# A slot's products ahead of the scores and its other stages behind them, and half-size products summed whole, in a fused encoder-decoder transformer layer

## The chip, the cores and the metric

The kernel runs on one core of one Trainium2 chip. The metric is the device time of one execution in microseconds (us); before the change it is 2730.48 us, the median of three runs (2728.22 to 2731.12).

The engines named below are PE (TensorE, matmuls and transposes through an identity), PEld (its weight loads, which overlap the matmuls), DVE (VectorE), ACT (ScalarE), POOL (GpSimd) and SP (the engine that issues all DMAs). Each works through its own instructions in the order in which the program gives them.

## The reference

One pre-norm transformer layer pair in float32. The encoder works on a short context (2 batches of 77 rows, 512 wide), the decoder on 2 batches of 2048 rows. Cut to what matters:

```python
memory = encoder(ctx)                      # 77 rows a batch
yn = ln(y, n1)
y = y + mha(yn, yn, sa_in, sa_out, causal bias)      # 16 heads of 32, 2048 x 2048 scores
y = y + mha(ln(y, n2), memory, ca_in, ca_out, bias)  # 2048 x 77 scores
y = y + relu(ln(y, n3) @ ff1.T + b1) @ ff2.T + b2    # 512 -> 2048 -> 512
def mha(xq, xkv, ...):
    scores = einsum("bhqd,bhkd->bhqk", q, k) / sqrt(32) + bias
    out = softmax(scores) @ v
    return out @ w_out.T + b_out
```

## The kernel before, in words

**Two stages.** The first stage, about the first 1640 us, is the decoder's causal self-attention; the encoder and the cross-attention of the first block of rows are spread out inside it. The second stage does cross-attention and the feed-forward part. The change touches the first stage alone.

**Blocks, units, pieces.** A block is a batch b and 512 of its rows, m = 0 to 3; the eight blocks are numbered x = 4b + m. A block has 16 units: four groups g of four heads times four tiles t of 128 query rows. A unit of m sees 4m + t + 1 key tiles of 128, which are cut into pieces of at most four tiles. So a unit of m = 1 has two pieces, and one of m = 2 or 3 three or four.

**One turn of the main loop** handles up to two pieces of one unit. On PE it is: `turn` transposes the unit's probabilities (L427, one PSUM bank for each key tile, copied out by ACT at L434 or by DVE at L432); if these pieces end unit n, `slot(n + 1)` does side work; one or two pieces of the scores of a later unit (`scores`, L375: four heads, a bank each; DVE empties each bank while it takes the row maximum, at L384 and L391, and L401 joins the maxima); and `values` (L456) multiplies the turned probabilities with v. The exponentials (L406) run on ACT.

**A slot's side work.** Three tables are filled ahead of the loop. `jobs` holds the products that make q, k, v of the next block and the output projection of the last one. In blocks with m > 0 these are Strassen-Winograd products of half size, numbered 1 to 7: `pair_job` for q (a and b are the two halves of the heads, so a25 is products 2 and 5) and `part_job` for k, v and o. `light` holds stages that ran ahead of the jobs: layer-norm statistics (L282 to L286) and centring, `norm_turn` (four transposes at L305 into one bank, emptied by four ACT instructions at L310), reciprocals of the softmax sums (L482, L484), loads, and for slots 65 to 98 the stages of the first block's cross-attention (L811, L836, L866, L874, L883 on PE; L845, L846 and L884 on DVE). `late` holds stages that ran behind the jobs: encoder stages, sums on POOL (L962), stores. Slots are counted here within a block, 0 to 15; slot s of block x is `slot(16x + s)`. Norms of the next block stand in slots 5 to 10, the output projection in slots 6 to 9, the next block's q and k products in slots 11 to 15.

**Eight banks.** PSUM has eight banks of 512 columns, handed out in a ring (`bank`): every product, each transposed key tile, each head of a score piece and each norm turn takes the next one. A matmul into a bank waits until the bank's last user has been read out. What PE may start therefore hangs on what stood eight banks before it in the program's order.

**What sets the order.** The scheduling is by hand: the order of the Python calls is the order on each engine.

**Sums of products.** Each half-size product leaves 128x512 in a bank, which is added onto one or two quarters of its result (DVE, or ACT for product 1). `last[0]` is true for the last job of a slot; its sums are made in two halves of 256 columns (L1150), those of the others whole (L1159, L1161, L1164).

Of the kernel before, what the change touches and what calls it, by code (L numbers as in the profile page):

```python
# [17 lines left out]
P = 128  # L18
# [36 lines left out]
def tile_encoder_decoder(ctx: ExitStack, tc: tile.TileContext, ins, out):  # L55
# [103 lines left out]
    with (  # L159
# [252 lines left out]
        def turn(pieces):  # L412
# [10 lines left out]
            for o, load in enumerate(loads):  # L423
# [608 lines left out]
        def pair_job(b, m, h, parts):  # L1032
# [8 lines left out]
            def run(w):  # L1041
# [3 lines left out]
                mm = bank()  # L1045
                for j, i in enumerate(parts):
                    n = of_nT(b, m, PARTS[i][1])
                    for c in range(2):
                        nc.tensor.matmul(mm[:, ts(j, TOK)], w[:, 2 * j + c, :], n[:, c, :], start=c == 0, stop=c == 1)  # L1049
# [3 lines left out]
                got = [mm[:, ts(j, TOK)] for j in range(len(parts))]  # L1053
                if parts == (1, 6):
                    ve.tensor_scalar(d["11"], got[0], qbias[:, 2 * h : 2 * h + 1], None, ALU.add)
                    ve.tensor_tensor(d["12"], got[1], d["11"], ALU.add)
                elif parts == (7, 4):
                    ve.scalar_tensor_tensor(d["22"], got[0], qstep[:, h : h + 1], d["12"], ALU.add, ALU.add)
                    ve.tensor_tensor(d["21"], got[1], d["22"], ALU.add)
                elif parts == (2, 5):  # L1060
                    for to, j in (("11", 0), ("12", 1), ("22", 1)):
                        ve.tensor_tensor(d[to], got[j], d[to], ALU.add)
                else:
                    assert parts == (3,)
                    ve.tensor_tensor(d["12"], got[0], d["12"], ALU.add)

            return load, run, True
        n_tiles, last = {}, [False]
# [4 lines left out]
        ADDS = {2: ("11",), 3: ("12",), 5: ("22", "12")}  # L1073
# [34 lines left out]
        def part_job(kind, b, m, i):  # L1108
# [20 lines left out]
            def run(w):  # L1129
                n, mm = of_o(b, m, by) if kind == "o" else of_nT(b, m, by), bank()  # L1130
                left, right = (w, n) if kind == "k" else (n, w)
                for f in range(2):
                    for c in range(2):
                        nc.tensor.matmul(  # L1134
                            mm[:, ts(f, TOK)], left[:, c, ts(f, P)], right[:, c, :], start=c == 0, stop=c == 1,
                        )
                got = mm.rearrange("p (f n) -> p f n", f=2)
                d = {to: place(to) for to in ("11", "12", "21", "22")}
                if i == 1 and kind == "k":
                    for f in range(2):  # L1140
                        nc.scalar.activation(
                            d["11"][:, f, :], got[:, f, :], AF.Identity, bias=vec("dec_sa_in_b", NC + f)
                        )
                elif i == 1:
                    nc.scalar.copy(d["11"], got)
                elif last[0] and not (i == 7 and kind == "k"):
                    for f in range(2):
                        for to in {6: ("12",), 7: ("22",), 4: ("21",)}.get(i) or ADDS[i]:
                            onto = {6: "11", 7: "12", 4: "22"}.get(i, to)
                            ve.tensor_tensor(d[to][:, f, :], got[:, f, :], d[onto][:, f, :], ALU.add)  # L1150
                elif i == 6:
                    ve.tensor_tensor(d["12"], got, d["11"], ALU.add)
                elif i == 7 and kind == "k":
                    for f in range(2):
                        ve.scalar_tensor_tensor(
                            d["22"][:, f, :], got[:, f, :], kstep[:, f : f + 1], d["12"][:, f, :], ALU.add, ALU.add
                        )
                elif i == 7:
                    ve.tensor_tensor(d["22"], got, d["12"], ALU.add)  # L1159
                elif i == 4:  # L1160
                    ve.tensor_tensor(d["21"], got, d["22"], ALU.add)  # L1161
                else:
                    for to in ADDS[i]:
                        ve.tensor_tensor(d[to], got, d[to], ALU.add)  # L1164
# [20 lines left out]
        late = {n: [] for n in light}  # L1185

        for x, (b, m) in enumerate(blocks):
# [13 lines left out]
            else:  # L1201
                todo = {
                    -5: "a16 a74", -4: "k1 k6", -3: "k7 k4", -2: "k2 a25", -1: "k5 k3 a3", 0: "v1 v6", 1: "v7 v4 v2",
                    2: "v5 v3", 3: "b16", 4: "b74 b25", 5: "b3",
# [789 lines left out]
```

## Time and profile before

| what | value |
|---|---|
| median of three runs | 2730.48 us |
| the profiled execution, its own time | 2728.59 us |
| its span, first to last instruction | 2726.8 us |
| self-attention stage | 0 to about 1640 us |
| block 1 (batch 0, m = 1) | 161 to 368 us |
| block 2 (m = 2) | 368 to 597 us |
| block 3 (m = 3) | 597 to 853 us |
| block 5 (batch 1, m = 1) | 989 to 1183 us |
| block 6 (m = 2) | 1183 to 1412 us |
| block 7 (m = 3) | 1412 to 1640 us |

In the timeline view a row has the start in us, the duration in us, the engine, the line and operation, what is written and read, the shapes and a count of merged instructions; in brackets stands idle time of the engine just before, and what ended it. A float32 matmul at L375, L456 or L1134 is two instructions in the trace, a transpose at L427 is one, so a score piece is eight rows of L375. In the view by windows each row is a stretch, its length, and then each engine's busy time and instructions.

### The profile page before, as it was taken

Reading aid. Unit: us, or ns where it says so; the run is one execution under the profiler, and the core shown is the slowest. Engines: PE = TensorE matmul, PEld = TensorE weight load, DVE = VectorE, ACT = ScalarE, POOL = GpSimd, SP = SyncE. Lnnn points to the kernel's source line nnn. Section 1 sums busy time; section 2 is a strip of 40 time slices with the busy share of each in tenths; the row PEclk is TensorE's granted clock in tenths of the full one; section 3 lists DMA queues with packets and bytes.
Section 4 is the critical chain, followed back from the end, with each engine's and each line's share of the span. In section 5 each row is a group of like instructions: output and inputs, shape, how many; then the busy total and the mean of one; then the engine's idle time right before and its main releaser. Section 6 shows DMA issues by size and latency. Waiting matters only on the chain.

```text
span 2726.8 us, 68267 instructions
## 1 busy us (share of the span) xinstructions
PE 2708.1 (99%) x26606; PEld 2217.9 (81%) x26606; DVE 1839.9 (67%) x5445; ACT 1537.0 (56%) x2978; POOL 1002.4 (37%) x844
## 2 busy tenths in 40 slices
PE   9999999999999999999999999999999999999998
PEld 6678877777876677777777777898989898989898
DVE  4776688888885677788888783646464746464645
ACT  3554567777786547667777784444444444444431
POOL 2612235500300513322300203455556565656456
PEclk9999999999999999999999999999999999999999
DMA  8724355511213522343311206565657565656465
GB/s 242 213 92 135 126 155 164 168 50 43 67 45 89 143 76 72 111 133 98 126 50 35 79 19 220 171 214 173 213 171 239 168 216 170 218 166 219 151 224 185
DMA packets 296277, 385.10 MB, mean 141 GB/s; under 512 B 41184, under 2 KB 165648, under 8 KB 295826
## 3 DMA queue, kind: packets, MB, share of 16 engines
q1 hardware_dynamic: 295954, 380.73, 44.1%
q8 instruction: 211, 3.46, 0.5%
q14 instruction: 112, 0.92, 0.1%
HBM read 334.15 MB, written 46.47 MB: 140 GB/s over the span
## 4 chain that ended last, share of the span: by engine, by line
PE 95%; DVE 1%; ACT 1%; DMA 1%; POOL 1%; issue 1%; SPq 0%; DVEq 0%; POOLq 0%; ACTq 0%
PE psum L427 18%; PE psum L1638 14%; PE psum L1667 13%; PE psum L375 11%; PE psum L456 9%; PE psum L1134 8%; PE psum L1801 3%; PE psum L1758 3%; PE psum L1049 3%; PE psum L866 2%; PE psum L836 1%; PE psum L874 1%; PE psum L590 1%; PE psum L811 1%; PE psum L239 1%; PE psum L215 1%
## 5 line engine op out<-in xcount | busy, mean ns | idle before, releaser
L406 ACT ACTIVATE pp<-pp,nm 128x128 f32<-128x128 f32 (+15 forms) x512 | 611.8, 1200 | 28.6 <-DVE nm L401 27.8
L384 DVE TENSOR_SCALAR_CACHE_REDUCE pp<-psum 128x512 f32<-128x512 f32 (+3 forms) x1024 | 556.2, 591 | 51.3 <-PE psum L375 49.7
L434 ACT COPY pts<-psum 128x512 f32<-128x512 f32 x714 | 384.1, 594 | 312.6 <-PE psum L427 265.6
L427 PE MATMUL psum<-ident,pp 128*128 128x128 f32 x4352 | 530.4, 277 | 4.7 <-ACT nT L310 4.0
L427 PEld LDWEIGHTS psum<-ident,pp 128*128 128x128 f32 x4352 | 474.0, 141 | 55.7 <-DVE pp L384 21.4
L375 PE MATMUL psum<-kT,q 32*128 32x512 f32 (+3 forms) x2560 | 336.5, 559 | 2.5 <-DVE q L217 1.0
L456 PEld LDWEIGHTS psum<-pts,vv 128*32 128x32 f32 x8704 | 226.4, 110 | 127.4 <-DVE pp L384 55.4
L1667 PE MATMUL psum<-pp 128*128 128x128 f32 x2560 | 304.5, 276 | 1.9 <-POOL pp L962 1.6
L1667 PEld LDWEIGHTS psum<-pp 128*128 128x128 f32 x2560 | 296.3, 192 | 8.6 <-issue 2.8
L432 DVE COPY pts<-psum 128x512 f32<-128x512 f32 x374 | 245.2, 685 | 82.6 <-PE psum L427 80.3
L456 PE MATMUL psum<-pts,vv 128*32 128x128 f32 x8704 | 279.6, 276 | 0.8 <-DVE mx L391 0.3
L962 POOL TENSOR_TENSOR pp<-pp 128x512 f32<-128x512 f32 x159 | 212.8, 1356 | 111.0 <-DMA pp<-in_dec_ff_wT_dram 50.6
L1638 PE MATMUL psum<-vv,pp 128*128 128x256 f32 x1024 | 236.2, 381 | 0.0
L375 PEld LDWEIGHTS psum<-kT,q 32*128 32x128 f32 x2560 | 146.3, 183 | 107.1 <-issue 41.3
L1638 PEld LDWEIGHTS psum<-vv,pp 128*128 128x128 f32 x1024 | 190.3, 190 | 25.8 <-issue 0.5
L391 DVE CUSTOM_DVE_ANT_0 pp<-psum,bias 128x256 f32<-128x256 f32 (+1 forms) x512 | 196.0, 411 | 19.7 <-PE psum L375 19.7
L1651 DVE TENSOR_TENSOR kT<-kT,psum 128x512 f32<-128x512 f32 x96 | 65.8, 686 | 191.6 <-PE psum L1638 191.4
L1654 ACT ACTIVATE kT<-kT,vecs 128x256 f32<-128x256 f32 x192 | 86.9, 501 | 156.6 <-DVE kT L1651 155.9
L1638 PE MATMUL psum<-nT,pp 128*128 128x256 f32 x768 | 174.1, 380 | 0.5 <-DVE oT L471 0.5
L1638 PEld LDWEIGHTS psum<-nT,pp 128*128 128x128 f32 x768 | 144.2, 190 | 20.8 <-issue 1.4
L1675 ACT COPY oT<-psum 128x128 f32<-128x128 f32 x56 | 15.0, 268 | 238.9 <-PE psum L1667 238.9
L494 POOL TENSOR_TENSOR oT<-rirows,oT 128x512 f32<-128x512 f32 x30 | 38.4, 1280 | 293.6 <-DMA rirows<-rec 181.7
(272 smaller groups left out, 4110.6 us busy)
## 6 DMA issues: line engine op xcount, KB each, us to landing
pp<-w_d SPq DMA_DIRECT2D x520, 256.0 KB
pp<-in_dec_ff_wT_dram SPq DMA_DIRECT2D x112, 256.0 KB
bias<-tzg SPq DMA_DIRECT2D x128, 128.0 KB
pp<-wo_d SPq DMA_DIRECT2D x56, 256.0 KB
wqk<-in_dec_sa_in_wT_dram SPq DMA_DIRECT2D x52, 256.0 KB
wqk<-sa_q SPq DMA_DIRECT2D x84, 128.0 KB
vv<-in_enc_ff_wT_dram SPq DMA_DIRECT2D x8, 1024.0 KB
xr<-in_x_dram SPq DMA_DIRECT2D x32, 256.0 KB
```

The source lines that it names most:

```text
L375: nc.tensor.matmul(banks[r][:, : kn * P], q[rows4(r), ts(t, P)], kT[rows4(r), g, k0 * P : (k0 + kn) * P], start=True, stop=True,)
L384: nc.vector.tensor_scalar(p[:, k0 : k0 + far], s[:, :far], 1.0, None, ALU.mult, ALU.max, accum_out=st["mx"][:, r, c : c + 1],)
L391: nc.vector.tensor_tensor_reduce(p[:, k0 + far : i + 1], s[:, far:kn], near[:, 2 - (kn - far) :], 1.0, LOWEST, ALU.add, ALU.max, accum_out ...
L406: nc.scalar.activation(p, p, AF.Exp, bias=nm, accum_out=to)
L427: nc.tensor.transpose(pt[:, ts(x, P)], state[n]["p"][r][:, k], ident)
L432: nc.vector.tensor_copy(pts[:, : len(load), :], pt[:, :w])
L434: nc.scalar.copy(pts[:, : len(load), :], pt[:, :w])
L456: nc.tensor.matmul(ot[rows4(r)], vv[:, k, ts(g * HC + r, HD)], got.pop((n, k, r)), start=k == k0 and (whole or not begun), stop=k == k1 - ...
L962: engine.tensor_tensor(out, a, b, ALU.subtract)
L1134: nc.tensor.matmul(mm[:, ts(f, TOK)], left[:, c, ts(f, P)], right[:, c, :], start=c == 0, stop=c == 1,)
L1638: nc.tensor.matmul(mm[:, ts(f, TOK)], a[:, c, ts(f, P)], b[:, c, :], start=fresh and f == 0 and c == 0, stop=c == 1, skip_group_check=True,)
L1667: nc.tensor.matmul(psum[:, bank_i, ts(col, P)], lhs[:, c, :], w[:, c, :], start=fresh and k in (0, 3) and c == 0, stop=c == 3, skip_group_ ...
```

## The change

Three things are done at once.

1. For units of blocks with m > 0, and for the slots 10 and 11 of the very first block (`parted`), the slot is taken apart. Its jobs (`products`) stay where they were, between `turn` and the scores; its `light` and `late` stages now follow the scores and stand ahead of `values`. One stage, the second part of a weight store (`w2_store(c, 1)`), goes with the products (`ahead`).
2. Every half-size product is summed whole, behind its four matmuls, also the last one of a slot. Both the q products and the others now take their sums from one table (`SUMS`); products 2 and 5 change places (a52 for a25, b52 for b25, output 5 ahead of 2), and k's product 2 goes behind the pair a52.
3. In a `turn` whose slot has no jobs (`direct`), DVE copies every other bank of the second half, where it copied all of the second half (or banks 4 and 6 of eight), and one group of exponentials stands ahead of another copy.

The core of the diff:

```diff
-                w = len(load) * P
+                w, half = len(load) * P, len(loads) // 2
-                if free or (o % 2 if first else o in (4, 6) if len(loads) == 8 else o >= (len(loads) + 1) // 2):
+                if free or (o % 2 if first else o >= half and (len(loads) - o) % 2 if direct else o in (4, 6) if len(loads) == 8 else o >= (len(loads) + 1) // 2):
...
-                if not first and o == (7 if len(loads) == 8 else min(3, len(loads) - 1)):
+                if not first and o == (max(0, len(loads) - 2) if direct else 7 if len(loads) == 8 else min(3, len(loads) - 1)):
...
+                mm = [bank()] * 2
...
-                elif last[0] and not (i == 7 and kind == "k"):
-                    for f in range(2):
-                        for to in {6: ("12",), 7: ("22",), 4: ("21",)}.get(i) or ADDS[i]:
-                            onto = {6: "11", 7: "12", 4: "22"}.get(i, to)
-                            ve.tensor_tensor(d[to][:, f, :], got[:, f, :], d[onto][:, f, :], ALU.add)
...
+                    else:
+                        for to, onto in SUMS[i]:
+                            ve.tensor_tensor(d[to][:, f], got[:, f], d[onto][:, f], ALU.add)
...
+                sums(slice(0, 2))
...
-                    -5: "a16 a74", -4: "k1 k6", -3: "k7 k4", -2: "k2 a25", -1: "k5 k3 a3", 0: "v1 v6", 1: "v7 v4 v2",
+                    -5: "a16 a74", -4: "k1 k6", -3: "k7 k4", -2: "a52 k2", -1: "k5 k3 a3", 0: "v1 v6", 1: "v7 v4 v2",
...
-                    for k, part in ((0, 1), (0, 6), (1, 7), (1, 4), (2, 2), (2, 5), (3, 3)):
+                    for k, part in ((0, 1), (0, 6), (1, 7), (1, 4), (2, 5), (2, 2), (3, 3)):
...
+        def products(n):
+            for f in ahead[n]:
+                f()
+            for _, run, _ in jobs[n]:
+                load_next()
+                run(loaded[ran[0]])
+                ran[0] += 1
+
         def slot(n):
             for f in light[n]:
                 f()
-            for k, (_, run, _) in enumerate(jobs[n]):
-                load_next()
-                last[0] = k == len(jobs[n]) - 1
-                run(loaded[ran[0]])
-                ran[0] += 1
+            products(n)
             for f in late[n]:
                 f()
...
-            light[u + k + 2].append(lambda c=c: w2_store(c, 1))
+            ahead[u + k + 2].append(lambda c=c: w2_store(c, 1))
...
-            turn(pair)
+            parted = ends and n + 1 < end and (units[n][1] > 0 or n in (9, 10))
+            turn(pair, parted and not jobs[n + 1])
...
-            if ends and n + 1 < end:
+            if parted:
+                products(n + 1)
+            elif ends and n + 1 < end:
                 slot(n + 1)
             if not third:
                 exps((0, 2, 1, 1)[units[n][1]])
...
+            if parted:
+                for f in light[n + 1] + late[n + 1]:
+                    f()
             if third and not ends:
                 exps(1)
             values(pair)
```

Over the program DVE gets 63 additions fewer, and seven copies out of PSUM go from DVE to ACT; PE, POOL and SP have the same instructions as before. New lines: the half-size products are L1053 for q (L1049 before) and L1161 for k, v and o (L1134 before), their sums L1157.

**PE in slot 5 of block 5**, from the turn to the values; L811 is a norm's turn, L883 the output projection and L836 the scores of the first block's cross-attention, L1049 the q product 3. Before:

```order
L427 MATMUL psum<-ident,pp 128x128 x20
L811 MATMUL psum<-ident,kT 128x128 x4
L883 MATMUL psum<-vv,kT 128x512 x4
L836 MATMUL psum<-pp 128x77 x16
L1049 MATMUL psum<-nT,wqk 128x256 x2
L375 MATMUL psum<-kT,q 128x384 x4
L375 MATMUL psum<-kT,q 128x512 x4
L456 MATMUL psum<-pts,vv 32x128 x20
```

Now:

```order
L427 MATMUL psum<-ident,pp 128x128 x20
L1053 MATMUL psum<-nT,wqk 128x256 x2
L375 MATMUL psum<-kT,q 128x384 x4
L375 MATMUL psum<-kT,q 128x512 x4
L811 MATMUL psum<-ident,kT 128x128 x4
L883 MATMUL psum<-vv,kT 128x512 x4
L836 MATMUL psum<-pp 128x77 x16
L456 MATMUL psum<-pts,vv 32x128 x20
```

The three cross-attention stages went from ahead of the product to behind both score pieces. On DVE the readings of their banks (L884, L845, L846) moved with them, from ahead of the sum of the q product to behind the last reading of the score banks.

**PE in slot 9 of block 2**, output product 3 and one norm turn. Before:

```order
L427 MATMUL psum<-ident,pp 128x128 x8
L305 MATMUL psum<-ident,xt 128x128 x4
L1134 MATMUL psum<-wqk,oT 128x256 x4
L375 MATMUL psum<-kT,q 128x384 x4
L375 MATMUL psum<-kT,q 128x512 x4
L456 MATMUL psum<-pts,vv 32x128 x8
```

Now:

```order
L427 MATMUL psum<-ident,pp 128x128 x8
L1161 MATMUL psum<-wqk,oT 128x256 x4
L375 MATMUL psum<-kT,q 128x384 x4
L375 MATMUL psum<-kT,q 128x512 x4
L305 MATMUL psum<-ident,xt 128x128 x4
L456 MATMUL psum<-pts,vv 32x128 x8
```

The norm turn, and with it a bank of the ring, went from ahead of the product to between the scores and the values.

**DVE in slot 8 of block 7**: the last copies of the turn, a group's reciprocals, the sums of output products 2 and 5, and the first reading of the scores. Before:

```order
L432 COPY pts<-psum 128x512 x2
L482 RECIPROCAL ri_110<-sums 128x16
L484 STREAM_TRANSPOSE rt<-ri_110 128x32
L1164 TENSOR_TENSOR wbig<-psum,wbig 128x2x256
L1150 TENSOR_TENSOR wbig<-psum,wbig 128x256 x4
L391 ISA pp,mx<-psum,bias 128x2x128
L391 ISA mx 128x1
```

Now:

```order
L432 COPY pts<-psum 128x512 x2
L1157 TENSOR_TENSOR wbig<-psum,wbig 128x2x256 x3
L391 ISA pp,mx<-psum,bias 128x2x128
L391 ISA mx 128x1
```

The sum of the last product was four additions of 256 columns (product 5, onto two quarters) and is one of 512 (product 2); the reciprocals moved to behind the readings of both score pieces.

More of the change, by code (lines that the diff above doesn't have):

```diff
@@ L410, in tile_encoder_decoder, with turn @@
         got = {}
-        def turn(pieces):
+        def turn(pieces, direct):
             first = units[pieces[0][0]][1] == 0
@@ L1072, in tile_encoder_decoder @@
         }
-        ADDS = {2: ("11",), 3: ("12",), 5: ("22", "12")}
         def of_nT(b, m, name):
@@ L1134, in run @@
                         nc.tensor.matmul(
-                            mm[:, ts(f, TOK)], left[:, c, ts(f, P)], right[:, c, :], start=c == 0, stop=c == 1,
+                            mm[f][:, ts(f, TOK)], left[:, c, ts(f, P)], right[:, c, :], start=c == 0, stop=c == 1,
                         )
-                got = mm.rearrange("p (f n) -> p f n", f=2)
-                d = {to: place(to) for to in ("11", "12", "21", "22")}
-                if i == 1 and kind == "k":
-                    for f in range(2):
[L1141 to L1145, printed above, removed]
-                elif last[0] and not (i == 7 and kind == "k"):
-                    for f in range(2):
-                        for to in {6: ("12",), 7: ("22",), 4: ("21",)}.get(i) or ADDS[i]:
-                            onto = {6: "11", 7: "12", 4: "22"}.get(i, to)
[L1150 to L1164, printed above, removed]
+                sums(slice(0, 2))
             return load, run, True
@@ L1184, in tile_encoder_decoder @@
         light = {n: [] for n in range(-1, len(units) + NU)}
-        late = {n: [] for n in light}
+        late, ahead = {n: [] for n in light}, {n: [] for n in light}
         for x, (b, m) in enumerate(blocks):
```

65 lines of the change are left out of this document (42 added, 23 removed).

## The prediction

> **What bounds the kernel now.** I read the page's busy times first, then the windows by block, then the score matmuls alone in the same windows, then the timeline at the places where these run long.
>
> ```profile
> PE 2708.1 (99%) x26606; PEld 2217.9 (81%) x26606; DVE 1839.9 (67%) x5445; ACT 1537.0 (56%) x2978; POOL 1002.4 (37%) x844
> 368.00:597.00 229.00, 228.90 (x2800) 178.42 (x2792) 190.05 (x649) 166.76 (x286) 86.42 (x72) 1.00 0.47 143
> 989.00:1183.00 194.00, 193.93 (x2056) 146.91 (x2048) 145.28 (x497) 128.84 (x266) 55.62 (x47) 0.99 0.29 90
> 1412.00:1640.00 228.00, 227.81 (x3036) 181.94 (x3038) 191.86 (x637) 180.81 (x269) 19.02 (x15) 1.00 0.16 51
> 1900.00:2000.00 100.00, 100.00 (x732) 91.16 (x731) 48.99 (x98) 43.09 (x94) 56.34 (x52) 1.00 0.59 194
> ```
>
> The last four rows are blocks 2, 5 and 7 and a piece of the feed-forward stage; their columns are PE, PEld, DVE, ACT, POOL, granted clock, DMA share, GB/s. PE shows no idle time anywhere, and all idle time of the run would be 2726.8 − 2708.1 = 18.7 us. But a matmul's recorded time covers its wait inside the pipeline: weight loads fill 91% of the feed-forward window and 76 to 80% of the blocks. So the blocks may hold waits that the busy time hides, while DVE is at 75 to 84%.
>
> The Trainium skill says the same of such traces ("Perfetto Trace Analysis", section "Identifying the Most-Contended Engine"): matmul busy time is a bad measure because matmuls are pipelined, the share of the weight loads a good one. By busy time alone at most 18.7 us could be won; by the page more, and the next rows agree with the page.
>
> ```profile
> 161.00:368.00 207.00, 33.74 (x272) 15.21 (x272) 1.00 0.39 123
> 368.00:597.00 229.00, 53.52 (x424) 23.03 (x424) 1.00 0.47 143
> 597.00:853.00 256.00, 59.51 (x448) 26.62 (x448) 1.00 0.15 47
> 989.00:1183.00 194.00, 42.05 (x272) 17.87 (x272) 0.99 0.29 90
> 1183.00:1412.00 229.00, 53.61 (x424) 23.03 (x424) 1.00 0.33 105
> 1412.00:1640.00 228.00, 57.55 (x432) 25.95 (x432) 1.00 0.16 51
> 495.16 2.00 PE L375 MATMUL psum<-kT,q 32*128 32x512 f32 x16
> 497.09 1.96 PE L456 MATMUL psum<-pts,vv 128*32 128x128 f32 x64
> 276.29 1.78 PE L375 MATMUL psum<-kT,q 32*128 32x384 f32 x16
> 278.01 1.30 PE L456 MATMUL psum<-pts,vv 128*32 128x128 f32 x40
> ```
>
> The first six rows are the score matmuls (L375) alone by block: PE, PEld. Blocks 1 and 5 run the same 272, and block 5 takes 8.3 us more. The last rows give the price without a wait, from a pair of pieces to the values behind it: 1.93 us for two full ones, 1.72 us for one of three tiles and one of four, so 0.108 to 0.121 us a row. By these the waits are 1 to 4 us in block 1, 9 to 13 in block 5, 2 to 8 in blocks 2 and 6 each, 6 to 11 in block 3 and 5 to 11 in block 7: 25 to 55 us in all. That is the pool from which this change can draw.
>
> **Part by part. The cross-attention stages of block 5.** Slot 5 before:
>
> ```profile
> 1043.34 3.60 PE L883 MATMUL psum<-vv,kT 128*128 128x512 f32 x8
> 1046.87 1.13 PE L836 MATMUL psum<-pp 32*128 32x77 f32 x32
> 1048.10 0.48 DVE L845 TENSOR_REDUCE cmx<-psum 128x4 f32<-128x308 f32 x1 [0.42 <-PE psum L836]
> 1048.99 4.37 PE L375 MATMUL psum<-kT,q 32*128 32x384 f32 x16
> 1052.11 0.28 DVE L384 TENSOR_SCALAR_CACHE_REDUCE pp<-psum 128x128 f32<-128x128 f32 x1
> 1053.30 1.30 PE L456 MATMUL psum<-pts,vv 128*32 128x128 f32 x40
> ```
>
> The scores run from 1048.99 to 1053.30, 4.31 us where 1.72 are needed: the last heads want the four banks of L836, which DVE empties from 1048.10 on, and DVE reads no score before 1052.11. Moved behind, the product and both pieces follow the turn at once, and DVE reads scores while PE does L883 (3.60 us) and L836 (1.13 us). These and the values (1.30) give DVE 6 us for the eight heads, so neither engine waits. Gain here 2.6 us. Slots 2 and 10 have the same shape. Of the 9 to 13 us in this block I take **9**.
>
> **Norm turns in front of the scores** stand in slots 7 to 10 of blocks 1, 2, 3 and 5. Slot 9 of block 2:
>
> ```profile
> 485.99 0.60 PE L305 MATMUL psum<-ident,xt 128*128 128x128 f32 x4
> 486.87 0.68 DVE L282 BATCH_NORM_STATS2 bnst<-xt 128x6 f32<-128x512 f32 x1
> 487.59 1.53 ACT L310 ACTIVATE nT<-psum,vecs 128x128 f32<-128x128 f32 x4
> 487.87 0.15 DVE L285 TENSOR_SCALAR rstd<-bnmv 128x1 f32<-128x1 f32 x1
> 488.25 2.77 PE L375 MATMUL psum<-kT,q 32*128 32x384 f32 x16
> 488.35 0.76 DVE L1150 TENSOR_TENSOR wbig<-psum,wbig 128x256 f32<-128x256 f32 x2 [0.33 <-PE psum L1134]
> 490.94 0.64 PE L456 MATMUL psum<-pts,vv 128*32 128x128 f32 x16
> ```
>
> The scores take 490.94 − 488.25 = 2.69 us, 0.97 over the 1.72 of such a pair: a head wants the norm turn's bank, which ACT frees at 489.12. Behind the scores it hinders none, so 0.97 is the upper end. The lower is what DVE gains, since the next turn's eight banks wait for its readings: it starts about 0.43 us earlier, PE's share of the norm turn (485.99 to the product at 486.42). Of twelve such slots in blocks 1 to 3 (block 5 is counted above), near the lower end because DVE is at 83% there: 12 × 0.43 = **5**.
>
> **The very first block, slots 10 and 11.** Here the turn itself waits for the norm's bank:
>
> ```profile
> 105.60 1.48 ACT L310 ACTIVATE nT<-psum,vecs 128x128 f32<-128x128 f32 x4
> 107.14 0.86 PEld L427 LDWEIGHTS psum<-ident,pp 128*128 128x128 f32 x8 [2.07 <-ACT nT L310]
> 113.11 1.29 PEld L427 LDWEIGHTS psum<-ident,pp 128*128 128x128 f32 x12 [2.44 <-ACT nT L310]
> ```
>
> L310 stands behind four exponentials on ACT, so transposes idle 2.07 and 2.44 us. With the norm turns behind the scores, four score banks come between, and the transposes pass; the copies on ACT are as late as before and give some of it back. Of 4.5 us I take **3** (bounds 0 and 4.5). Block 1's encoder stages leave 1 to 4 us of waits; I take **1.5**.
>
> **Sums whole.** Slot 8 of block 3:
>
> ```profile
> 723.09 0.69 DVE L1164 TENSOR_TENSOR wbig<-psum,wbig 128x512 f32<-128x512 f32 x1 [0.60 <-PE psum L1134]
> 724.64 0.74 PEld L375 LDWEIGHTS psum<-kT,q 32*128 32x128 f32 x14 [0.33 <-ACT nT L310]
> 724.82 1.42 DVE L1150 TENSOR_TENSOR wbig<-psum,wbig 128x256 f32<-128x256 f32 x4 [1.03 <-PE psum L1134]
> ```
>
> The halves were meant to start before the product ends, and do not: the first starts at 724.82, behind all its matmuls, after DVE idled 1.03 us. So one whole sum loses nothing and takes 0.69 us for 0.76 (63 × 0.07 = 4.4 us of DVE, hidden; counted at 0). The new order counts for more: behind the last product stands product 2's 0.69 us in place of product 5's 1.42, so DVE reaches the scores 0.73 us earlier. That shows where the scores wait for it: two such slots of m = 3, and partly the slots 14 (k2 behind a52). I take **2.5** (bounds 0 and 5).
>
> The page "PSUM — Partial Sum Buffer" of the Trainium skill (section "PSUM bank collisions raise a hardware error") says to guard PSUM by bank, not by address; by this rule no half can be read while PE fills the other, and the 1.03 us agree. If halves could start early, the change would cost up to 0.38 us at each such sum.
>
> **What it costs.** Before, DVE did the statistics in front of the sums, in time in which it waited for products. Now they follow eight score readings and stand ahead of the next turn's copies.
>
> ```profile
> L282 DVE BATCH_NORM_STATS2 bnst<-xt 128x6 f32<-128x512 f32 x24 | 16.2, 675 | 0.0
> L482 DVE RECIPROCAL ri<-sums 128x16 f32<-128x16 f32 x28 | 6.8, 242 | 0.0
> 1122.20 1.03 PE L1049 MATMUL psum<-nT,wqk 128*128 128x256 f32 x4
> 1117.39 1.28 POOL L962 TENSOR_TENSOR xr<-nT,xt 128x512 f32<-128x512 f32 x1
> ```
>
> One set is 1.15 us (486.87 to 488.02), 24 sets 28 us. They are hidden while DVE has slack before the next scores; at 83% of a turn of about 14 us it has 2.4. Bounds 0 and 28; I charge a fifth, **5**, because DVE's idle time is spread. POOL's token sums for slot 11 start later too: the last of them ended at 1118.67, 3.5 us before the first q product at 1122.20, and out of the moved scores come 2 to 4 us; I charge **1**. SP's loads for the products now stand ahead of the slot's other DMAs, which can only help them; nothing is counted. The seven copies that go to ACT cost it 0.59 instead of 0.69 on DVE, nothing on the path.
>
> **Sum:** 9 + 5 + 3 + 1.5 + 2.5 − 5 − 1 = 15 us gained. The profiled execution (2728.59 us; its span is 1.8 less) would come to 2713.6; the median of the runs stands 1.9 above it, so I forecast 2730.5 − 15 = **2715 us**, with a range of its own of 2706 to 2722.
>
> **Rivals.** (a) *DVE sets the pace.* Where PE saves a wait, the ring makes it wait again for DVE in the next turn. For it: DVE at 83 to 84% in blocks 2, 3, 6 and 7, and the 0.43 against 0.97 above. Against it: block 5 has DVE at 75% and the largest waits. If only half of block 5's 9 and 3 of the rest stay, less 2.5 of the costs, it is 5 us: 2725.
>
> (b) *The moved statistics are exposed: slower.* One mechanism, on DVE between the last score reading and the first copy of the next turn. It decides from the point where the readings still queued when the values start, plus 1.15, outlast the values and the first four transposed tiles (1.96 + 1.8 us). Exposed in blocks 2, 3 and 6 are 12 sets of 1.15 and some 18 reciprocals with their transposes of 0.45, 22 us; the 5 and 2.5 are not gained, and of the other 13.5 all stay: 22 − 13.5 + 1 = +9.5, 2740 us. For it: eight readings of 0.61 are 4.9 us. Against it: half of them are done when the values start.
>
> (c) *More is freed.* If the pool of 25 to 55 us goes by half or more, 30 us: 2700. For it: every wait that the timeline shows has a moved stage or a sum in front. Against it: DVE's share.
>
> (d) *It does nothing to the time*, the waits only changing their place: it lies at the upper end of (a).
>
> **How the numbers follow.** Forecast 0.52, (a) and (d) 0.22, (b) 0.18, (c) 0.08. A measurement of this kernel can tell about 0.2%, 5.5 us. Faster by more: 0.52 + 0.08 and half of (a), 0.70; within: the rest of (a) and a little of (b), 0.14; slower 0.16. The range of 2702 to 2733 leaves out the far ends of (b) and (c), about 0.2.
>
> **What would show it.** In the changed trace the score matmuls of block 5 take about 33 us where they took 42.05, those of blocks 2 and 6 some 51; slot 5 of block 5 has 1.7 us from scores to L811; no transposes wait 2 us at 105 to 113 us; DVE starts one sum of 512 about 0.2 us behind each product. I am wrong if transposes of the turn (L427) or the values (L456) take up what the scores give back, as (a) and (b) say, or if slot 11 of block 5 waits for POOL's sums.

## The result and the profile after

| | median, us | lowest to highest | runs |
|---|---|---|---|
| before | 2729.44 | 2724.54 to 2731.12 | 17 |
| the change | 2734.56 | 2731.89 to 2740.71 | 17 |

The ratio, of runs on the same chips, is 1.0026 with a 95% interval of 1.0019 to 1.0032: the change is slower by 7 us (0.0026 × 2729.4; the two medians alone lie 5.1 apart), where 15 us of gain were forecast. The span of the profiled execution is 2732.5 us, 5.7 more than before.

The gain that was forecast can be seen at its place. The page's first row of the change, and the score matmuls alone (L375) in blocks 2, 3 and 5, first of the change, then of before in the same stretches (from a block's start to the next; columns PE, PEld, granted clock, DMA share, GB/s):

```profile
PE 2702.4 (99%) x26606; PEld 2207.8 (81%) x26606; DVE 1831.7 (67%) x5375; ACT 1540.4 (56%) x2985; POOL 1001.8 (37%) x844
```

```profile
369.00:591.00 222.00, 51.23 (x408) 21.89 (x408) 1.00 0.49 147
591.00:855.00 264.00, 58.62 (x464) 26.52 (x464) 1.00 0.16 46
993.00:1188.00 195.00, 35.26 (x272) 15.88 (x272) 0.99 0.29 87
```

```profile
369.00:590.00 221.00, 51.07 (x408) 21.76 (x402) 1.00 0.48 145
590.00:854.00 264.00, 61.51 (x464) 27.51 (x464) 1.00 0.15 48
```

In block 5 the scores take 35.26 us where they took 42.05 (forecast: about 33). In block 2 they take what they took (51.2 and 51.1; the forecast of 51 was set against the 53.52 of a longer stretch, which holds 16 rows more), in block 3 2.9 us less. Yet block 5 as a whole, from the score piece in front of its first turn (989.09 before, 993.47 now) to that of block 6 (1183.14 and 1188.20), takes 194.7 us and took 194.1. PE's busy time fell by 5.7 us and its span grew by 5.7: so there are new idle times, and these, unlike the hidden waits of before, stand in the timeline as gaps with a releaser. Block by block, from the last values of one block to the last of the next, the change's trace is longer by 3.1 us in block 1, 1.2 in blocks 2 and 6 each, 3.1 in block 4 and 0.7 in block 5, and shorter by 2.4 in the very first block, 0.5 in block 3 and 0.7 in block 7.

**Slot 11 of block 5**, where PE makes the q products from POOL's token sums:

```profile
1095.18 0.56 POOL L286 TENSOR_TENSOR rstd<-rstd,mhalf 128x1 f32<-128x1 f32 x1 [6.72 <-DVE rstd L285]
1100.55 2.90 SPq L1113 DMA_DIRECT2D y<-xr  x2
1110.08 1.14 SPq L262 DMA_DIRECT2D xr<-in_x_dram  x2
1114.24 1.28 POOL L1111 TENSOR_TENSOR xr<-xr,row_dec_sa_out_b 128x512 f32<-128x512 f32 x1 [2.34 <-DMA xr<-in_x_dram]
1117.74 1.03 PE L1053 MATMUL psum<-nT,wqk 128*128 128x256 f32 x4
1119.42 1.27 POOL L962 TENSOR_TENSOR xt<-nT 128x512 f32<-128x512 f32 x1
1122.09 1.13 PE L1053 MATMUL psum<-xt,wqk 128*128 128x256 f32 x4 [3.32 <-POOL xt L962]
1123.33 3.68 PE L1053 MATMUL psum<-xr,wqk 128*128 128x256 f32 x8
```

PE idles 3.32 us, and loses about 1.8 more inside the xr products (3.68 us for 1.89); the 1.8 are clock, which was granted at 0.50 from 1123.40 to 1126.80 (last section). The chain back: POOL's sums (L962) stand behind its additions to the output (L1111); these wait for the residual's load (L262), which SP issues at 1110.08, behind the stores (L1113) that waited for POOL's additions of the slot before, and behind ten more DMAs that it issues between the two; and those additions stand on POOL behind a norm (L286) that waits for DVE's statistics.

But the chain is hardly later than before. Counted from the first transposes of the block's first turn (989.74 before, 995.45 now), POOL's first sum for this slot starts at 123.8 us before and at 124.0 now. It is PE that comes earlier, to the slot's first product at 122.3 us where it came at 132.5: the block's gain is there (some 1.7 us of the 10.2 are a halved clock before), and it ends at a chain that did not move along.

In slot 7 the norm, in front of a sum that PE needs:

```profile
1070.02 0.55 POOL L286 TENSOR_TENSOR rstd<-rstd,mhalf 128x1 f32<-128x1 f32 x1 [17.02 <-DVE rstd L285]
1073.61 1.27 POOL L962 TENSOR_TENSOR oT<-oT,xr 128x512 f32<-128x512 f32 x1
1074.93 1.99 PE L1161 MATMUL psum<-wqk,oT 128*128 128x256 f32 x8 [1.76 <-POOL oT L962]
```

POOL stood still for 17 us in front of L286 and made the sum only then; PE waits 1.76 us for it. POOL stood as long before (17.75 us), but there the norm began 70.2 us behind the first transposes and now at 74.6, while PE comes to the products of slot 7 at 75.8 us where it came at 81.3.

**Slot 3 of block 4**, a block whose slots the change does not take apart except slot 0. First the change, then before:

```profile
854.88 0.21 DVE L484 STREAM_TRANSPOSE rt<-ri 128x32 f32<-128x32 f32 x1
855.12 2.66 SPq L487 DMA_DIRECT2D rec<-rt  x4
873.03 7.29 SPq L199 DMA_DIRECT2D wqk<-in_dec_sa_in_wT_dram  x3
874.86 5.06 PE L215 MATMUL psum<-nT,wqk 128*128 128x512 f32 x8 [3.65 <-DMA wqk<-in_dec_sa_in_wT_dram]
```

```profile
848.17 0.21 DVE L484 STREAM_TRANSPOSE rt<-ri 128x32 f32<-128x32 f32 x1
848.41 2.66 SPq L487 DMA_DIRECT2D rec<-rt  x4
867.16 6.59 SPq L199 DMA_DIRECT2D wqk<-in_dec_sa_in_wT_dram  x3
869.75 3.60 PE L215 MATMUL psum<-nT,wqk 128*128 128x512 f32 x8
```

A reciprocal and its transpose, 0.45 us of DVE, were put behind the readings of the scores and end 6.7 us later, of which 1.3 are the later start of the block on PE (the product L226 of slot 0 starts at 848.76 for 847.47). SP's store of them (L487) waits so much longer, all loads behind it in SP's order move with it, and the weights of L215 come late: PE idles 3.65 us, and the product takes 5.06 for 3.60 at a clock granted at 0.50 from 874.3 to 877.7. No score is in this chain.

### The profile page after: what moved, and what is told of

It reads as the page before. It is cut to its first block, busy times and chain, and to the rows that moved or that the text cites. A ratio compares the mean times of both kernels' runs of the same rounds, so it can differ in the third digit from the quotient of the medians.

```text
span 2732.5 us, 68220 instructions
## 1 busy us (share of the span) xinstructions
PE 2702.4 (99%) x26606; PEld 2207.8 (81%) x26606; DVE 1831.7 (67%) x5375; ACT 1540.4 (56%) x2985; POOL 1001.8 (37%) x844
## 4 chain that ended last, share of the span: by engine, by line
PE 91%; DVE 2%; issue 2%; DMA 2%; ACT 2%; POOL 1%; SPq 1%; POOLq 0%; DVEq 0%; ACTq 0%
PE psum L427 17%; PE psum L1642 14%; PE psum L1671 12%; PE psum L375 10%; PE psum L456 9%; PE psum L1161 8%; PE psum L1805 3%; PE psum L1762 3%; PE psum L1053 2%; PE psum L866 2%; PE psum L836 1%; ACT pp L406 1%; PE psum L590 1%; PE psum L874 1%; PE psum L811 1%
## 5 line engine op out<-in xcount | busy, mean ns | idle before, releaser
L375 PE MATMUL psum<-kT,q 32*128 32x512 f32 (+3 forms) x2560 | 324.4, 558 | 2.8 <-ACT kT L231 1.4
L962 POOL TENSOR_TENSOR pp<-pp 128x512 f32<-128x512 f32 x159 | 212.8, 1356 | 117.0 <-DMA pp<-in_dec_ff_wT_dram 49.1
L375 PEld LDWEIGHTS psum<-kT,q 32*128 32x128 f32 x2560 | 142.0, 183 | 101.6 <-issue 37.6
L494 POOL TENSOR_TENSOR oT<-rirows,oT 128x512 f32<-128x512 f32 x30 | 38.4, 1280 | 342.9 <-DMA rirows<-rec 340.0
```

The lines of the kernel that those rows point to most:

```text
L375: nc.tensor.matmul(banks[r][:, : kn * P], q[rows4(r), ts(t, P)], kT[rows4(r), g, k0 * P : (k0 + kn) * P], start=True, stop=True,)
L962: engine.tensor_tensor(out, a, b, ALU.subtract)
```

## The experiments

Theories: **Q**, the moved stages hold up what stands behind them in the order of POOL and SP; **S**, the prediction's rival (b): the moved statistics are exposed on DVE between the scores and the next turn; **S2**, the whole sums cost time; **E**, the encoder's stages of block 1 are better ahead of the scores. A ratio is to the kernel before on the same chip.

**Slot 0 of block 4 alone in the old order** (e1_slot64).

```diff
-parted = ends and n + 1 < end and (units[n][1] > 0 or n in (9, 10))
+parted = ends and n + 1 < end and n != 63 and (units[n][1] > 0 or n in (9, 10))
```

> The change, but slot 0 of block 4 (behind unit 63) is issued in the old order: light stages, products, late ones, and then the scores. Theory Q (queues: the moved stages hold up what stands behind them in SP's and POOL's order): SP issues the stores of the reciprocals (L487) some 6 us earlier again, L215 in slot 3 of block 4 no longer waits 3.65 us for its weights, and the time falls by about 5 us against the change, to 2729-2730, ratio to before 1.000. Rival C (that wait was the chance of one execution): the median stays at 2734-2735, ratio 1.002-1.003. Rival S (the loss comes from the moved statistics on DVE or from the whole sums): also 2734-2735.

Measured: 2731.72 us, ratio 1.0010 (1.0001 to 1.0019). The wait is gone:

```profile
851.52 2.66 SPq L487 DMA_DIRECT2D rec<-rt  x4
872.86 3.60 PE L215 MATMUL psum<-nT,wqk 128*128 128x512 f32 x8
```

So 0.0016, 4.4 us, hang on one place where 0.45 us of DVE were moved. In this run's trace the unit is 5.3 us shorter than in the change's: 3.65 of idle time, and the rest the slower product.

**All stages without a matmul in front again** (e2_early).

```diff
+for f in light[n + 1]:
+    if f in early:
+        f()
 products(n + 1)
...
-for f in light[n + 1] + late[n + 1]:
+for f in [f for f in light[n + 1] if f not in early] + late[n + 1]:
```

`early` holds the reciprocals with their stores, loads and multiplies, the statistics, the centring, `out_done` and `load_bias`.

> The change, but of the light stages those that hold no matmul or transpose stay in front of the products: the reciprocals with their stores, loads and multiplies, the loads of the biases, the statistics and centring of the norms, and the additions and stores of the attention's output. Norm turns, cross-attention and encoder stages and the late stages stay behind the scores. Theory Q: the waits at slot 3 of block 4 (5 us) and slots 10 and 11 of block 5 (5 us) go, the gains of block 5 and of the very first block stay: 2722-2726, ratio 0.998. Rival S (statistics exposed on DVE where they are moved): they are in front again here, so another 3 to 5 us below that, 2718-2721. If neither holds: 2733-2736.

Measured: 2722.89 us, ratio 0.9979 (0.9970 to 0.9988), as theory Q had it: 13 us below the change, with every norm turn and every cross-attention stage still behind the scores.

The lengths of the units in the two traces (from a unit's first transpose to the next unit's) agree to 0.6 us throughout self-attention, except in six places. There the change takes 5.3 us more in slot 3 of block 4, 2.0 and 1.5 in slots 7 and 11 of block 5, and 0.8, 1.0 and 0.8 in the units with slot 7 of blocks 2, 3 and 6. The first three are the waits shown above (in slot 11 e2_early still waits 2.17 us). The last three are another thing, theory S's. In block 2, in the change:

```profile
453.28 0.68 DVE L282 BATCH_NORM_STATS2 bnst<-xt 128x6 f32<-128x512 f32 x1
454.29 0.28 DVE L471 TENSOR_TENSOR oT<-psum,oT 128x128 f32<-128x128 f32 x1
454.62 0.66 PE L427 MATMUL psum<-ident,pp 128*128 128x128 f32 x4 [0.55 <-DVE oT L471]
```

The statistics stand between DVE's last reading of the scores and L471, for whose bank PE's transposes wait. So S is there, at three of the twelve places in blocks 2, 3 and 6 where it was to be, and is worth 2.6 us in all; at the other nine the moved statistics cost nothing.

**Only the sums** (e3_sums).

```diff
-parted = ends and n + 1 < end and (units[n][1] > 0 or n in (9, 10))
+parted = False
-ahead[u + k + 2].append(lambda c=c: w2_store(c, 1))
+light[u + k + 2].append(lambda c=c: w2_store(c, 1))
```

> Only the whole sums and the new order of two products; every slot is issued in the old order. The prediction's term: 2.5 us gained, 2727, ratio 0.999. Theory Q: within 1.5 us of before (2728-2731). Rival S2 (whole sums cost time, since DVE begins later or holds the banks longer): 2732-2735, ratio above 1.001.

Measured: 2725.47 us, ratio 0.9991 (0.9982 to 1.0000): 2.5 us, the prediction's term (the interval reaches from 0 to 5). S2, above 1.001, falls.

**The statistics and the rest apart** (e4_queues, e11_stats). In e2_early two groups went to the front. Each alone, with the same code and a shorter list: reciprocals, biases and out_done,

> As the run with the stages without a matmul in front, but the statistics and the centring of the norms stay behind the scores, so DVE's statistics are moved and SP's stores, the reciprocals and POOL's additions to the output are not. Theory Q: 2724-2728; the SP wait at slot 3 of block 4 is gone, POOL's sums of slot 11 of block 5 are late by less than in the change. Rival S: 3 to 5 us above the run with the statistics in front.

and statistics with centring,

> The change with only the statistics and centring of the norms (DVE, POOL) kept in front of the products; reciprocals, their stores, biases, and the additions and stores of the attention's output stay behind the scores. With the change (ratio 1.0026), e4_queues (1.0010) and e2_early (0.9979) it makes a square. Theory Q, POOL's part: PE's waits for POOL's sums (oT 1.76 us in slot 7, xt 3.3 us in slot 11 of block 5) shrink, and slot 0 of block 4 with its 5 us remains: 2728-2730, ratio 0.9995 to 1.001. Rival S, statistics exposed on DVE: the same time, but then the waits at POOL's sums remain and the transposes behind the values (L427) shorten in blocks 2 and 3.

| in front of the products | ratio | interval |
|---|---|---|
| none (the change) | 1.0026 | 1.0019 to 1.0032 |
| reciprocals, biases, out_done | 1.0010 | 1.0002 to 1.0019 |
| statistics, centring | 1.0060 | 1.0048 to 1.0073 |
| both | 0.9979 | 0.9970 to 0.9988 |

The first, 2729.99 us, lies above the 2724 to 2728 of theory Q: it is no better than the experiment on slot 0 of block 4 alone. It is 7 us above e2_early, which is also more than S's 3 to 5; of the six places that of block 4 is gone in its trace, and the other five are as long as in the change or longer. The second misses both theories: 2728 to 2730 were expected, and it took 2745.01. What was overlooked is POOL's order. With the statistics in front, POOL's norm stands ahead of the output's additions and waits there for DVE's statistics, which come behind the turn's copies:

```profile
1106.82 0.56 POOL L286 TENSOR_TENSOR rstd<-rstd,mhalf 128x1 f32<-128x1 f32 x1 [11.97 <-DVE rstd L285]
1112.19 2.91 SPq L1113 DMA_DIRECT2D y<-xr  x2
1122.10 1.23 SPq L262 DMA_DIRECT2D xr<-in_x_dram  x2
1126.11 1.26 POOL L1111 TENSOR_TENSOR xr<-xr,row_dec_sa_out_b 128x512 f32<-128x512 f32 x1 [10.48 <-DMA xr<-in_x_dram]
1133.89 2.07 PE L1053 MATMUL psum<-xt,wqk 128*128 128x256 f32 x4 [9.90 <-POOL xt L962]
```

The additions end late, the store of their result (L1113) waits for them on SP, the next residual's load (L262) stands behind that store and ten more DMAs, the next additions wait 10.48 us for it, the token sums stand behind these, and PE idles 9.9 us. So the time rose with the statistics in front, though S's three places are as short there as in e2_early. The two groups do not add up, because each waits for the other in POOL's and SP's order.

**The token sums and their norm turn in front too**, on e2_early (e5_sums_early).

```diff
-light[turned_at].append(lambda b=b, m=m, t=t, on=on: norm_turn(b, m, t, on=on))
+turned = lambda b=b, m=m, t=t, on=on: norm_turn(b, m, t, on=on)
+light[turned_at].append(soon(turned) if x > 1 and t == 3 else turned)
...
-    lambda b=b, m=m, tag=tag: token_sums(b, m, tag)
+    soon(lambda b=b, m=m, tag=tag: token_sums(b, m, tag))
```

> As the run with the stages without a matmul in front (e2_early), and in slots 10 of the blocks the last norm turn with the token sums that POOL makes of it also stays in front. Theory Q: what e2_early still loses in slot 11 of block 5 (PE waits 2.17 us for xt and about 1 us within the xr products) goes: 3 us below it, 2719-2720, ratio 0.997. Rival T (the turn in front of the scores costs there what it cost before, 2 us of score waits): as e2_early, 2722-2723.

Measured: 2729.72 us, ratio 1.0005 (0.9996 to 1.0013), 7 us above e2_early: a miss, and on the far side of rival T. From one turn to the next, slot 11 of block 5 did get 3.3 us shorter, but slot 10 of that block got 4.7 us longer (some 2.5 of it clock, granted at 0.80 over that turn), and slot 10 of blocks 1 and 3 2.2 and 2.1 us. In block 1:

```profile
285.31 1.99 PE L375 MATMUL psum<-kT,q 32*128 32x512 f32 x14
288.67 1.12 PE L375 MATMUL psum<-kT,q 32*128 32x512 f32 x2 [1.37 <-ACT nT L310]
```

The last head wants the norm turn's bank, and ACT frees it (L310) only between two pairs of exponentials. So a norm turn ahead of the scores does cost what the prediction named, in a slot that has no product.

**Block 1 in the old order, and both edits together**, each on e2_early (e6_block1, e7_both).

```diff
-parted = ends and n + 1 < end and (units[n][1] > 0 or n in (9, 10))
+parted = ends and n + 1 < end and (units[n][1] > 0 and n // 16 != 1 or n in (9, 10))
```

> As e2_early, but the whole of block 1 (units 16 to 31) is issued in the old order. Theory E (the encoder's stages behind the scores let DVE's evictions L584 and with them the next transposes come late): block 1 gives back its 2.7 us, 2720, ratio 0.997. By the prediction's term, block 1 was to gain 1.5 us: 2724-2725.

> Both edits of the two runs above together. Theories Q and E: 6 us below e2_early, 2716-2718, ratio 0.9955. If one falls: 2719-2721.

Measured: 2721.37 us, ratio 0.9969 (0.9958 to 0.9980), for block 1 alone, 2.7 us below e2_early by the ratios (the intervals overlap; in the traces block 1 is 3.1 us shorter); both together 2725.22 us, 0.9983 (0.9975 to 0.9992), a miss with the same cause as the last. Why block 1 loses stands in its slot 2, first the change, then before:

```profile
180.97 2.58 PE L427 MATMUL psum<-ident,pp 128*128 128x128 f32 x20
184.15 0.66 PE L427 MATMUL psum<-ident,pp 128*128 128x128 f32 x4 [0.60 <-DVE pp L584]
185.21 0.66 PE L427 MATMUL psum<-ident,pp 128*128 128x128 f32 x4 [0.41 <-DVE pp L584]
187.53 2.09 PE L375 MATMUL psum<-kT,q 32*128 32x256 f32 x16
```

```profile
185.22 3.35 PE L427 MATMUL psum<-ident,pp 128*128 128x128 f32 x28
190.13 4.36 PE L590 MATMUL psum<-pp,vv 128*128 128x154 f32 x32
194.43 1.52 PE L375 MATMUL psum<-kT,q 32*128 32x256 f32 x16
```

DVE's emptying of the encoder's transposes (L584) now follows the score readings, and the next turn waits for it twice; and the scores, which had the encoder's 4.36 us of matmuls (L590) between the q products and themselves, now follow the products at once and take 2.09 us for 1.52, because DVE is still at the products' sums.

**Products first in block 5 alone** (and in the two slots of the first block; e8_block5), with the edits of e5_sums_early.

```diff
-parted = ends and n + 1 < end and (units[n][1] > 0 or n in (9, 10))
+parted = ends and n + 1 < end and (n // 16 == 5 or n in (9, 10))
```

> Products first only in block 5 and in slots 10 and 11 of the very first block, with the stages without a matmul, the token sums and their norm turn in front; blocks 1, 2, 3, 6 and 7 in the old order. If the norm turns behind the scores in blocks 2 and 3 are worth the prediction's 0.43 us each, this is 4 us above e7_both; if they are worth nothing, within 1 us of it, 2716-2718.

Measured: 2722.53 us, ratio 0.9971 (0.9959 to 0.9982). Neither 2716 to 2718 nor a time of 4 us above the version with all blocks came out: it is 3 us below that one, so the norm turns of blocks 2 and 3 did not show a worth; that version also paid for its norm turn in slot 10 of block 3, so this alone settles it only roughly. The next pair is cleaner.

**The residuals' loads ahead** (e9_load_first, e10_block5_load). Block 1 in the old order, no token sums in front, but the last two residuals' loads right behind the store that frees their buffers; and the same with block 5 alone.

```diff
-late[out_at + 2 + k // 2].append(lambda b=b, m=m, k=k: residual_load(b, m, k))
+load = soon(lambda b=b, m=m, k=k: residual_load(b, m, k))
+(light[out_at + 3] if k >= 2 else late[out_at + 2]).append(load)
```

> As e6_block1, and the loads of the last two residuals of a block (SP, L262) are issued behind the store that frees their buffers and ahead of the reciprocals' stores, where they stood some 7 us later. Theory Q: POOL's additions then run before nT is there, its token sums follow nT at once, and the 2 to 5 us that slot 11 of block 5 loses go: 3 us below e6_block1, ratio 0.9955 to 0.996. Rival W (SP, which now waits for the store to end, brings the reciprocals and weights late instead): 0.997 or above.

> Products first only in block 5 and in slots 10 and 11 of the very first block, all stages without a matmul in front, and the residuals' loads ahead as in e9_load_first. If products first is worth nothing in blocks 2, 3, 6 and 7, it is within 0.0006 of e9_load_first; if the norm turns there are worth the prediction's 0.43 us each, 0.0015 above it.

Measured: 2715.88 us, ratio 0.9954 (0.9941 to 0.9968), and 2715.98 us, 0.9954 (0.9941 to 0.9966). Both beat both kernels. In the first one slot 11 of block 5 reads:

```profile
1088.06 2.73 SPq L262 DMA_DIRECT2D xr<-in_x_dram  x2
1095.80 1.27 POOL L1111 TENSOR_TENSOR xr<-xr,row_dec_sa_out_b 128x512 f32<-128x512 f32 x1
1101.65 1.28 POOL L962 TENSOR_TENSOR xt<-nT 128x512 f32<-128x512 f32 x1 [0.62 <-ACT nT L310]
1105.33 1.03 PE L1053 MATMUL psum<-xt,wqk 128*128 128x256 f32 x4
1106.19 1.89 PE L1053 MATMUL psum<-xr,wqk 128*128 128x256 f32 x8
```

These additions no longer wait for the load, POOL's sums follow nT at once, 117.5 us behind the first transposes and so earlier than before too, and PE does not idle. Block 5, counted as above, takes 187.1 us (982.21 to 1169.27) where it took 194.1, of which some 1.7 are clock (0.99 over the 194 us before, 1.00 now). And with blocks 2, 3, 6 and 7 in the old order the time is the same. The intervals alone would leave room for some 5 us either way; the traces do not: with products first blocks 2 and 6 are 0.4 us longer, block 3 is 0.4 shorter and block 7 the same. Products first is worth nothing there.

**The very first block in the old order**, on that version (e12_first_old, taken from e9_load_first).

```diff
-parted = ends and n + 1 < end and (units[n][1] > 0 and n // 16 != 1 or n in (9, 10))
+parted = ends and n + 1 < end and units[n][1] > 0 and n // 16 != 1
```

> As e9_load_first, but slots 10 and 11 of the very first block in the old order. By the prediction's term they are worth 3 us (bounds 0 and 4.5): ratio 0.9965, with PE waiting 2 us for nT (L310) in front of two turns again. Rival: what is won there is spent at the next product, whose weights (sa_k) SP brings when it can, whatever PE does before: within 0.0005 of e9_load_first (0.9954).

Measured: 2718.55 us, ratio 0.9966 (0.9952 to 0.9979), 0.0012 above the version it is taken from: 3.3 us by the medians, the prediction's 3, though the intervals overlap. The two waits stand in its trace again:

```profile
106.89 0.85 PEld L427 LDWEIGHTS psum<-ident,pp 128*128 128x128 f32 x8 [2.07 <-ACT nT L310]
112.87 2.03 PEld L427 LDWEIGHTS psum<-ident,pp 128*128 128x128 f32 x12 [2.44 <-ACT nT L310]
```

From the values of unit 8 to those of unit 13 the three traces in the old order take 41.3 to 42.4 us and the eleven in the new one 38.4 to 41.1, 2 us less on average (in two of the three a halved clock behind the second wait is part of it). The rival holds in part: in five of the eleven PE waits 1.4 to 1.9 us for the weights sa_k at the product behind (L1161).

The third part of the change, the copies shared between DVE and ACT, goes with the slots that are taken apart in every run here; what it is worth by itself was not measured.

## Why the prediction was wrong

The sign was wrong; three of its gains were there, two of them with an open size.

- **Cross-attention stages of block 5, 9 us: right in mechanism and nearly in size.** Slot 5 of the change runs as forecast:

```profile
1047.83 1.78 PE L375 MATMUL psum<-kT,q 32*128 32x384 f32 x16
1049.55 0.66 PE L811 MATMUL psum<-ident,kT 128*128 128x128 f32 x4
```

  1.72 us from the scores to L811, where they took 4.31. The units with slots 2, 5 and 10 are 1.5, 2.5 and 3.0 us shorter (the last holds about 1 us of halved clock before). With the new waits taken away, block 5 gains 7.0 us, 5.3 without the clock.
- **The very first block, 3 us: right in mechanism**, both waits are gone; the size is open (3.3 by medians whose intervals overlap, 2 by the traces). **The sums, 2.5 us: right** within a wide interval (2.5, from 0 to 5); they start right behind the product, see the next rows.
- **Norm turns, 5 us: wrong, worth nothing.** Slot 9 of block 2 after the change, in which the norm turn stands behind the scores:

```profile
487.75 1.89 PE L1161 MATMUL psum<-wqk,oT 128*128 128x256 f32 x8
489.57 2.76 PE L375 MATMUL psum<-kT,q 32*128 32x384 f32 x16
489.68 0.69 DVE L1157 TENSOR_TENSOR wbig<-psum,wbig 128x512 f32<-128x512 f32 x1 [0.97 <-PE psum L1161]
```

  The scores take 2.76 us, as they took 2.77. The step read their 0.97 us of delay as a wait for the norm turn's bank. It is a wait for DVE, which comes to the scores only after the product's sum (489.68 to 490.37), with the norm turn in front or not. This was rival (a), DVE sets the pace, at one kind of place. (The prediction also left out block 6, which has four such norm turns; it gains nothing either.) Where no product stands in the slot the norm turn's bank does decide, as e5_sums_early shows.
- **Block 1, a gain of 1.5: wrong, a loss of some 2.7** (3.1 in the traces). The encoder's stages were the cover under which DVE summed the products; the step asked only which waits leave.
- **What it costs, 5 + 1 us: the step that failed.** It priced the moved statistics as time of DVE, "SP's loads for the products now stand ahead of the slot's other DMAs, which can only help them; nothing is counted", and POOL's delay as 1 us. DVE's time was 2.6 us of the price, at three places. The larger part came from the instructions in these stages that other engines wait for: DVE's reciprocals, for which SP's store waits with the next weights behind it (0.0016, 4.4 us, at one place), and DVE's statistics, for which POOL's norm waits with the sums behind it. And the 3.5 us by which POOL's sums were ready were counted to the product's old time, 1122.20, while the same prediction brought PE forward by 9 us in this block: PE came 10.2 us earlier, the sums did not, and PE waits 3.32 us. Taking statistics, reciprocals and additions to the front and then the residuals' loads won 0.0031 and 0.0015 more, 8.5 and 4.1 us. The prediction did name "if slot 11 of block 5 waits for POOL's sums" as a sign of being wrong, and that wait is the largest in the block.
- **Rival (b), statistics exposed on DVE: right in sign, an eighth of its size.** It put 22 us into blocks 2, 3 and 6; the traces show 2.6 there.

Put together from the runs: −2.5 (sums) −3.3 (first block) −7.0 (block 5) +4.4 (SP at block 4) +8.5 and +4.1 (POOL and SP, the 4.1 a wait that the block's own gain laid bare) +2.7 (block 1) = +6.9 us, where 7 were measured; and the three gains alone, −12.8, against 0.0046 × 2729, 12.6, of the best version. The terms have intervals of some 2.5 us each, and the 7.0 of block 5 are from two single traces and hold 1.7 of clock, so the fit is better than they warrant. Of the 8.5 the traces place 2.6 in blocks 2, 3 and 6.

By the Trainium skill ("PSUM — Partial Sum Buffer", section "Engine vs sequencer instructions") the queues of ScalarE, VectorE and GpSimd are strict first in, first out; the 17.02 us of POOL in front of L286 agree: the sum behind it had its operands from POOL by 1053.01, and its place was free when PE's product of slot 6 ended at 1060.62. SP's order behaves likewise here.

## What to carry to other kernels

Before a stage is moved, list not its cost but who waits for its results on other engines, and what is queued behind the waiting instruction there; 0.45 us of DVE, moved by some 5 us, cost PE 5 through a store on SP. Count the slack of a result against the time at which its user will come after the change, not before it. Split a stage by engine: work without a matmul that feeds POOL or SP keeps its early place, and only what takes PSUM banks goes behind the scores, where a trace shows scores waiting for those banks. And a gain found at one kind of place (a cross-attention stage in front of the scores) is to be checked at the others for which engine ends the wait, before it is multiplied by their number.

## What was not expected of the hardware

The granted clock dipped between 75 and 100 us in some executions and not in others, with the same code at that place. First e2_early, then e6_block1, rows of the windows (PE, PEld, DVE, ACT, POOL, granted clock, DMA share, GB/s):

```profile
75.00:100.00 25.00, 23.47 (x235) 13.23 (x228) 22.46 (x77) 13.86 (x35) 20.30 (x14) 1.00 0.88 243
```

```profile
75.00:100.00 25.00, 23.35 (x212) 13.68 (x213) 19.94 (x63) 11.07 (x27) 17.14 (x12) 0.86 0.85 222
```

Between the same two products (L215, from 71.08 to 88.45 and from 71.35 to 92.76) lie 17.4 us at a clock of 1.00 and 21.4 at 0.86. That is more than half of what the whole change is worth, so a term of the very first block can't be read from single traces. By the Trainium skill ("TensorE: Matmul & The Clock Gate", section "Part 1: The HAM clock gate (the "warmup" mystery)") the clock is halved or full by how busy TensorE has been of late, judged in windows of some 3.4 us that run freely; one halved window in 25 us would make 0.93 and two 0.86, an estimate with which the 0.93 of before, the 0.86 here and the 1.00 of others agree.

The traces agree with the first part: the clock falls where PE has waited. In e6_block1 PE waits 1.50 us for DVE (L217) up to 78.05, and the clock is halved from 78.2; e2_early lacks that wait. The change in slot 3 of block 4 and slot 11 of block 5, where PE waited 3.65 and 3.32 us:

```profile
874.30:877.70 3.40, 2.84 (x4) 1.31 (x5) 0.00 (x0) 0.00 (x0) 1.86 (x2) 0.50 0.54 158
1123.40:1126.80 3.40, 3.40 (x8) 2.38 (x8) 0.84 (x2) 0.00 (x0) 3.40 (x3) 0.50 0.46 146
```

Between 130 and 1640 us the fourteen traces have nine idle times of PE of over 2 us, from 2.17 to 9.90, and the clock is at 0.50 for 3.4 us or more at the end of each, or within 2 us of it; behind shorter ones it is so in some traces only. By these traces a wait cost up to 1.7 us more than itself (half of 3.4) for each such stretch, which is the 5.06 for 3.60 and the 3.68 for 1.89 above. The dips at 976 to 984 us in six traces stand behind no such wait, and no run was made to try the cause.
